# Conv-attention hybrid with a recurrence: the last half image in written order, and the recurrence on the attention loop's PSUM banks

## The chip, the cores and the metric

The kernel runs on one core of a Trainium2 chip. The metric is device time in microseconds (us) of one execution. A core has five engines with a queue each: TensorE (matmuls and transposes, PE in the profile; its weight loads are PEld), VectorE (DVE), ScalarE (ACT), GpSimd (POOL) and SyncE (SP), whose queue issues the transfers here. Matmuls write to PSUM[...]; all else lies in SBUF or in device memory.

## The reference, cut to what matters

The input x is four images of 128 channels by 64 x 64 pixels. There are two layers of attention and then a recurrence.

- Layer 0: group norm over x; queries, keys, values and a gate from 1x1 convolutions; softmax attention over the 4096 pixels; the result times the gate, projected, added to x.
- Layer 1: the pixels as 4096 tokens of 128 values. `q = LN(t) @ W`, scores `q @ q.T` (symmetric), softmax, product with LN(t), added to t.
- Recurrence: `Wx = LN(t) @ W.T`, batch norm over all tokens of all images, then `y = sigmoid(wx + y @ V.T)` over the tokens in order; y is added to t, and t goes out as an image.

The batch norm needs the mean and variance over all tokens. So the recurrence can't start before the last tokens of the last image have their Wx.

## The kernel before, in words

Everything is fp32. `fast` does the work; `general` is a slower path taken only when a check at the end fails, and it doesn't run in these measurements. An image is cut into `NB = 8` blocks of 512 tokens.

**Layer 1** (`layer1`) goes through the blocks in the order 6, 7, 5, 4, 3, 2, 1, 0. For block n it computes scores against the blocks a = n, n-1, ..., 0 only, in two steps i of 256 tokens each: scores (L685), exponential on ScalarE (L689), products with LN(t) (`direct`, L564), two steps behind. In the step with a = n and i = 1 half of the scores are had by transposing earlier ones (`quarter`, L537, L543, L547, L551). Since the scores are symmetric, the exponentials for a < n are also transposed (L692 on VectorE, then 16 transfers, L719) and used for block a (`reversed_products`, L577). Each partial sum is added into `oacc` on VectorE (`part`, L586). When block n has all its parts, `finish(n)` requests the old tokens (L614) and puts closures into a queue `pending`:

- `tokens`: four transposes on TensorE (L619), row sums and reciprocal (L622 to L624), the addition to the old tokens (L626), and a layer norm (`layernorm`: L294 and L295 for each quarter, `inv_sqrt` on GpSimd with L140 and L141, then L298);
- `turn`: four transposes (L639), a copy on ScalarE (L640), and `result` (transposition L270 and four transfers, L274) for the new tokens;
- `inputs`: a matmul (L648), its statistics for the batch norm (L649) and a copy into `wxs` (L652).

One closure is taken from the queue per step of the loop. For the last image, block 0 takes block 1's part directly (`order`, `turns`), so its two a are 0 and 1, and no transposed scores are needed there. At the end `flush()` runs what is left.

**PSUM.** In the loop three pools share the eight banks: `ps_s` (2 tiles of 2 banks, scores), `ps_o` (3 banks, products) and `ps_m` (1 bank, the closures). One closure with a tile in `ps_m` must have been read out before the next can write there. Block 0 of the last image takes banks of `ps_s` instead. Then the pools close, and `ps_r` with six banks opens for the recurrence.

**The recurrence** starts from 128 places at once, 32 tokens apart, each with W = 12 tokens of run-in, for the two halves of the images in turn: 44 steps. At each step VectorE writes `gain * wx` into a bank two steps ahead (`preload`, L838; three banks per half in turn), TensorE adds `V y` to it (L851), and ScalarE takes the sigmoid with the bias (L855). Step 0 needs no matmul (L848). [...]each bank is first marked with a matmul (L815) whose value doesn't matter. Ahead of it stand the batch norm's sums (L819, `inv_sqrt`, L821 to L824). From step 15 on VectorE also adds y to the tokens (L865, one per step), and after the last step the four images go out (L870). The checks follow: sums in range (`ok`, L794 to L796, placed before the recurrence) and the run-in long enough (`gap`, L874 to L877).

**Order.** The kernel is written in a layer that places the waits itself and plans the order of the instructions on each engine from estimated times. What is written earlier tends to go first, but an instruction that isn't ready in the plan is passed by later ones.[...] `tc.keep_in_program_order` pins single instructions. `tc.manual_schedule()` keeps everything inside it in written order on each engine; work written ahead of it can still be mixed in by the planner.

Of the kernel before, what the change touches and what calls it, by code (L numbers as in the profile page):

```python
# [23 lines left out]
NT = N // P  # L24
EPS_GN, EPS_LN, EPS_BN = 1e-5, 1e-5, 1e-5
# [4 lines left out]
QB = 512  # L30
NB = N // QB
# [5 lines left out]
G = N // L  # L37
GB = QB // L


DEN_LO, DEN_HI = 2.0**-60, 2.0**100
# [4 lines left out]
SQ, BQ, SK, BK, SG, BG, GAMMA, BETA = range(8)  # L46
# [121 lines left out]
def fast(  # L168
# [13 lines left out]
    with ExitStack() as st:  # L182
# [2 lines left out]
        accp = st.enter_context(tc.tile_pool(name="accp", bufs=1))  # L185
        work = st.enter_context(tc.tile_pool(name="work", bufs=1))
        stat = st.enter_context(tc.tile_pool(name="stat", bufs=4))
        ps_s = st.enter_context(tc.tile_pool(name="ps_s", bufs=2, space=PSUM))
        ps_o = st.enter_context(tc.tile_pool(name="ps_o", bufs=3, space=PSUM))
        ps_m = st.enter_context(tc.tile_pool(name="ps_m", bufs=1, space=PSUM))  # L190

# [13 lines left out]
        def flush(until=None):  # L205

            while pending and until not in done:
                pending.popleft()()
# [75 lines left out]
            nc.sync.dma_start(dst, via)  # L284

        n_moves = 0

        def layernorm(src, dst):
# [21 lines left out]
        def quarters(t):  # L310
            return [t[:, j, :].rearrange("q (p i) -> q p i", p=4) for j in range(NQ)]
# [198 lines left out]
        def layer1(b, h, qt):  # L510

            oacc = big.tile([P, NB, QB], F32, tag="oacc", name="oacc")
# [80 lines left out]
            def finish(n):  # L595
                cs = bass.ts(n, QB)
                rinv = stat.tile([P, NQ], F32, tag="rinv", name="rinv")
                t = work.tile([P, 4, NQ, 32], F32, tag="t", name="t1", bufs=2)
                if b == B - 1 and n == 0:

                    one, two = (ep.tile([P, 2, QB], F32, tag="e", name="last") for _ in range(2))
                    h2, t1 = (one[:, r, :].rearrange("q (j c) -> q j c", j=NQ) for r in range(2))
                    th = two[:, 0, :]

                    def bank():
                        return ps_s.tile([P, 2, QB], F32, tag="s", name="ml")[:, 0, :]
                else:
                    h2 = work.tile([P, NQ, C], F32, tag="h2", name="h2")
                    th = work.tile([P, QB], F32, tag="th", name="th")
                    t1 = work.tile([P, NQ, C], F32, tag="og", name="t1b")  # L610

                    def bank():
                        return ps_m.tile([P, QB], F32, tag="m", name="m1")
                nc.sync.dma_start(t, t_d[b, n])  # L614

                def tokens():
                    m = bank().rearrange("q (j c) -> q j c", j=NQ)
                    for j in range(NQ):
                        nc.tensor.transpose(m[:, j, :], oacc[:, n, bass.ts(j, P)], ident)  # L619
                    at = (B + b) * NT + n * NQ  # L620
                    den = den_all[:, at : at + NQ]
                    nc.vector.tensor_reduce(den, m, AX.X, ALU.add)  # L622
                    nc.vector.tensor_scalar(den, den, 1.0 / C, None, ALU.mult)
                    nc.vector.reciprocal(rinv, den)  # L624
                    for j in range(NQ):
                        nc.vector.scalar_tensor_tensor(  # L626
                            t1[:, j, :].rearrange("q (p i) -> q p i", p=4),
                            m[:, j, :].rearrange("q (p i) -> q p i", p=4), rinv[:, j : j + 1],
                            t[:, :, j, :], ALU.mult, ALU.add,
                        )  # L630
                    layernorm(quarters(t1), quarters(h2))

                def result():
                    turn_out(t1.rearrange("q j (p i) -> q j p i", p=4), t2_d[b, :, cs])

                def turn():
                    m = bank()
                    for j in range(NQ):
                        nc.tensor.transpose(m[:, bass.ts(j, P)], h2[:, j, :], ident)  # L639
                    nc.scalar.copy(  # L640
                        th.rearrange("c (p j k) -> c j p k", j=NQ, p=4),
                        m.rearrange("c (j p k) -> c j p k", j=NQ, p=4),
                    )
                    result()

                def inputs():
                    m = bank()
                    nc.tensor.matmul(m, lhsT=wt["f"], rhs=th, start=True, stop=True)  # L648
                    nc.vector.bn_stats(bn_st[:, b * NB + n, :], m)  # L649
                    m = m.rearrange("p (g i s) -> p i g s", i=L // 2, s=2)  # L650
                    if b == B - 1:
                        nc.vector.tensor_copy(wxs[:, :, b, bass.ts(n, GB), :], m)  # L652
                    else:
                        wx = work.tile([P, L // 2, GB, 2], F32, tag="wx", name="wx")
                        nc.vector.tensor_copy(wx, m)
                        nc.sync.dma_start(wxs_d[b, :, :, bass.ts(n, GB), :], wx)

                if b == B - 1 and n == 0:
                    pending.appendleft(tokens)
                    pending.extend([turn, inputs])  # L660
                elif b == B - 1 and n < 4:
                    pending.extend([tokens, turn, inputs])
                else:
                    pending.extend([tokens, nothing, nothing, nothing, turn, inputs])


            for n in [NB - 2, NB - 1] + list(range(NB - 3, -1, -1)):
                o = None
                flush((b, n))
                if n == NB - 2:  # L670
                    queries(n)
# [51 lines left out]
            while fifo:  # L723
                direct()
            pending.extend([reversed_products] * len(turned))

        def own_bank(_):
            return ps_m.tile([P, 512], F32, tag="m", name="mp")
# [44 lines left out]
        for b in range(B):  # L773
# [13 lines left out]
            while ahead:  # L787
                ahead.popleft()()
        flush()


        tc.keep_in_program_order(nc.scalar.activation(first_y, shift, AF.Sigmoid))
        ok = big.tile([P, 2, 2 * B * NT], F32, tag="oacc", name="ok")
        nc.vector.tensor_scalar(ok[:, 0, :], den_all, DEN_LO, None, ALU.is_ge)  # L794
        nc.vector.tensor_scalar(ok[:, 1, :], den_all, DEN_HI, None, ALU.is_le)
        nc.vector.tensor_reduce(par_ok[:, 1:2], ok.rearrange("p a b -> p (a b)"), AX.X, ALU.min)  # L796


    with ExitStack() as st:
        scan = st.enter_context(tc.tile_pool(name="scan", bufs=1))  # L800
        ps_r = st.enter_context(tc.tile_pool(name="ps_r", bufs=1, space=PSUM))
# [9 lines left out]
        HB = B // 2  # L811
        banks = [[ps_r.tile([P, 512], F32, tag=f"r{s}{i}", name="ps_r") for i in range(3)] for s in range(2)]
        for s in range(2):
            for i in range(3):
                nc.tensor.matmul(  # L815
                    banks[s][i][:, : HB * G], lhsT=ident, rhs=wxs[:, 0, :HB, :, 0],
                    start=True, stop=True, skip_group_check=True,
                )
        nc.vector.bn_aggr(mv, bn_st.rearrange("p a b -> p (a b)"))  # L819
        inv_sqrt(gain, mv[:, 1:2], EPS_BN)  # L820
        nc.vector.tensor_mul(gain, gain, col(GAMMA))  # L821

        nc.vector.tensor_mul(bias, mv[:, 0:1], gain)
        nc.vector.tensor_sub(bias, col(BETA), bias)  # L824
# [18 lines left out]
        for k, i in enumerate(steps):  # L843
# [15 lines left out]
            if k >= W:  # L859
                todo.extend((i - 3, b) for b in range(B) if i % 4 == 3)  # L860
                for j in range(len(todo) if i == L - 1 else min(1, len(todo))):
# [7 lines left out]
                    if i0 == L - 4:  # L869
                        nc.sync.dma_start(out[b], t2[:, b, :])  # L870


        gap = scan.tile([P, B, G - 1], F32, name="gap")
        nc.vector.tensor_sub(gap, state[:, :, 1:G], at(y, L - 1, slice(0, B))[:, :, : G - 1])  # L874
# [406 lines left out]
```

## Time and profile before

| | us |
|---|---|
| median of 3 runs | 3050.52 (3049.5 to 3051.89) |
| span of the profiled run | 3049.4 |
| TensorE busy | 2991.0 (98%) |
| VectorE busy | 1676.6 (55%) |
| last attention product ends (L564) | 2945.1 |
| last inputs matmul (L648) | 2957.4 to 2959.5 |
| marks of the six banks (L815) | 2960.9 to 2966.1 |
| recurrence's matmuls (L851) | 2966.0 to 3022 |
| output transfers issued (L870) | from 3023.2 |
| end | 3049.4 |

Times in the lower half are positions in the span. The profile lists busy time per engine, the granted TensorE clock and the share of the transfer engines by stretch of the span, and a timeline of instructions with the idle time of the engine before each and what ended it.

### The profile page before, as it was taken

How to read it: one execution, taken by the hardware profiler on the slowest of the kernel's cores; microseconds unless marked ns; L12 is line 12 of the kernel's file. 1: busy time of each engine (PE TensorE's matmuls, PEld its weight loads, DVE VectorE, ACT ScalarE, POOL GpSimd, SP SyncE). 2: the span in 40 equal slices, each digit the busy share in tenths (PEclk: the TensorE clock that was granted, in tenths of full speed). 3: DMA queues.
4: the chain of work that ended last, by engine and by line, in shares of the span. 5: the costliest groups of instructions: out<-in, count | busy, mean ns of one | idle time of the engine just before them, and what ended most of it. 6: DMA issues, size and time to landing. Idle time of an engine off the chain costs nothing.

```text
span 3049.4 us, 31514 instructions
## 1 busy us (share of the span) xinstructions
PE 2991.0 (98%) x10716; PEld 1370.4 (45%) x10716; DVE 1676.6 (55%) x3114; ACT 1032.5 (34%) x1149; POOL 218.4 (7%) x215
## 2 busy tenths in 40 slices
PE   8999999999999999999999999999999999999985
PEld 4444444444444444444444444444444444444442
DVE  6666654434666664443466665443456666333356
ACT  3444432222344433222244443222234443222224
POOL 0011100000011100000011011000001111000000
PEclk9999999999999999999999999999999999999988
DMA  1112143434111123343311114343422112544333
GB/s 42 38 56 56 48 116 88 96 88 101 45 56 56 44 87 97 91 101 84 89 45 56 39 49 117 85 98 89 99 59 56 42 49 88 144 99 103 96 115 155
DMA packets 247562, 241.09 MB, mean 79 GB/s; under 512 B 90080, under 2 KB 162272, under 8 KB 246368
## 3 DMA queue, kind: packets, MB, share of 16 engines
q1 hardware_dynamic: 247392, 238.98, 29.4%
q8 instruction: 88, 1.44, 0.2%
q14 instruction: 82, 0.67, 0.1%
HBM read 65.80 MB, written 56.62 MB: 40 GB/s over the span
## 4 chain that ended last, share of the span: by engine, by line
PE 93%; DVE 3%; SPq 2%; ACT 1%; DMA 1%; issue 0%; POOL 0%; DVEq 0%; ACTq 0%
PE o L437 28%; PE o L564 15%; PE ps L233 14%; PE ps L685 14%; PE ot L577 12%; SPq L719 2%; PE m L262 1%; PE m L648 1%; PE mp L400 1%; PE ps L537 1%; PE mp L365 1%; PE mq L529 1%; PE mp L385 1%; DVE t2s L865 1%; DVE ps_r L838 1%; PE m L639 1%
## 5 line engine op out<-in xcount | busy, mean ns | idle before, releaser
L437 PE MATMUL o<-e,nxt 64*128 64x512 f32 x4096 | 972.9, 589 | 0.0
L235 ACT ACTIVATE e<-ps 128x1024 f32<-128x1024 f32 x512 | 521.6, 1025 | 688.7 <-PE ps L233 646.7
L242 DVE TENSOR_TENSOR acc<-acc,e 128x1024 f32<-128x1024 f32 x448 | 547.0, 1221 | 231.3 <-ACT e L235 215.0
L437 PEld LDWEIGHTS o<-e,nxt 64*128 64x128 f32 x4096 | 403.3, 187 | 483.0 <-issue 474.2
L233 PE MATMUL ps<-nxt 64*128 64x512 f32 x2048 | 542.4, 595 | 2.0 <-DVE nxt L377 0.9
L564 PE MATMUL o<-e,h 128*128 128x512 f32 x1160 | 537.0, 592 | 0.0
L689 ACT ACTIVATE e<-ps,shift 128x1024 f32<-128x1024 f32 x258 | 287.4, 1114 | 646.6 <-PE ps L685 357.1
L685 PE MATMUL ps<-qt 128*128 128x512 f32 x1032 | 482.9, 594 | 2.7 <-ACT qt L530 2.7
L577 PE MATMUL ot<-tt,h 128*128 128x512 f32 x888 | 400.9, 593 | 0.0
L692 DVE STREAM_TRANSPOSE dd<-e 128x512 f32<-128x512 f32 x444 | 281.7, 682 | 138.0 <-ACT e L689 103.0
L564 PEld LDWEIGHTS o<-e,h 128*128 128x128 f32 x1160 | 218.8, 190 | 268.3 <-issue 268.0
L233 PEld LDWEIGHTS ps<-nxt 64*128 64x128 f32 x2048 | 198.2, 187 | 232.0 <-issue 148.5
L685 PEld LDWEIGHTS ps<-qt 128*128 128x128 f32 x1032 | 189.9, 190 | 219.3 <-issue 190.3
L577 PEld LDWEIGHTS ot<-tt,h 128*128 128x128 f32 x888 | 167.8, 190 | 210.2 <-issue 205.1
L586 DVE TENSOR_TENSOR oacc<-oacc,ot 128x512 f32<-128x512 f32 x87 | 59.7, 686 | 288.2 <-PE ot L577 288.2
L140 POOL TENSOR_SCALAR rstd<-mv 128x4 f32<-128x4 f32 x64 | 14.6, 228 | 2380.0 <-DVE mv L295 2380.0
L491 DVE SCALAR_TENSOR_TENSOR t<-yt,rinv,t 128x128 f32<-128x128 f32 x128 | 36.4, 346 | 77.4 <-DMA yt<-turn_d 77.4
L502 POOL TENSOR_SCALAR h<-h 128x512 f32<-128x512 f32 x32 | 72.4, 2261 | 63.8 <-DVE d L270 61.7
L454 POOL TENSOR_SCALAR xb<-xb,bpc 128x512 f32<-128x512 f32 x32 | 59.1, 1846 | 245.0 <-DMA xb<-in_x_dram 211.5
L547 ACT ACTIVATE e<-ps,shift 128x512 f32<-128x512 f32 x32 | 22.0, 687 | 143.8 <-PE ps L543 126.3
L141 POOL TENSOR_TENSOR rstd<-rstd,mhalf 128x4 f32<-128x4 f32 x64 | 66.4, 1037 | 5.3
L588 DVE COPY oacc<-ot 128x512 f32<-128x512 f32 x24 | 16.6, 692 | 85.1 <-PE ot L577 85.0
(156 smaller groups left out, 1609.1 us busy)
## 6 DMA issues: line engine op xcount, KB each, us to landing
tt<-dd SPq DMA_DIRECT2D x1776, 64.0 KB, 2.0
turn_d<-d SPq DMA_DIRECT2D x384, 64.0 KB, 1.8
xb<-in_x_dram SPq DMA_DIRECT2D x32, 256.0 KB, 3.2
t<-turn_d SPq DMA_DIRECT2D x32, 256.0 KB, 2.7
yt<-turn_d SPq DMA_DIRECT2D x32, 256.0 KB, 2.6
t_d<-t SPq DMA_DIRECT2D x32, 256.0 KB, 2.0
qt<-turn_d SPq DMA_DIRECT2D x32, 256.0 KB, 2.9
t<-t_d SPq DMA_DIRECT2D x32, 256.0 KB, 3.0
```

Of the source, the lines that this page charges most:

```text
L141: nc.gpsimd.tensor_tensor(dst, dst, mhalf[:, :n], ALU.pow)
L233: nc.tensor.matmul(ps[:, h, :], lhsT=lhsT, rhs=rhs, start=True, stop=True)
L235: nc.scalar.activation(e, ps, AF.Exp, scale=scale)
L242: nc.vector.tensor_tensor(acc, acc, e, ALU.add)
L437: nc.tensor.matmul(o[r], lhsT=v[rs, p + h * PAIRS, :], rhs=e[rs, h, :], start=(p == 0 and h == 0), stop=(p == PAIRS - 1 and h == 1),)
L502: nc.gpsimd.tensor_scalar(hn, hn, 1.0, None, ALU.add)
L564: nc.tensor.matmul(o, lhsT=h[:, NQ * a + 2 * i + half, :], rhs=e[:, half, :], start=(a == order(n)[0] and i == 0 and half == 0), stop=(a = ...
L577: nc.tensor.matmul(ot, lhsT=h[:, NQ * n + j, :], rhs=t[:, :, j, :, :].rearrange("q p k j -> q k p j"), start=(j == 0), stop=(j == NQ - 1),)
L685: nc.tensor.matmul(ps[:, half, :], lhsT=qt[:, bass.ts(at, P)], rhs=qt[:, bass.ts(n, QB)], start=True, stop=True,)
L689: nc.scalar.activation(e, ps, AF.Exp, bias=shift)
L692: nc.vector.transpose(d.rearrange("q f b k j -> q k b f j")[:, 2 * i + half], e[:, half, :].rearrange("q (b f j) -> q b f j", b=NQ, f=NQ),)
L719: nc.sync.dma_start(t[bass.ts(f, 32), p], d[bass.ts(p, 32), f])
```

## The change

It has four parts.

1. From block 0 of the last image on, and through the recurrence, everything is put in written order (`tc.manual_schedule`). For block 1 an empty closure is put between `tokens` and `turn`.
2. The three PSUM pools live until the end, and the recurrence takes its six banks from them. Four are marked in block 0's `tokens`, while VectorE and GpSimd work on the layer norm; two after the last `inputs`, followed by three wider matmuls of the same kind, which keep TensorE busy. Block 0's closures take banks of `ps_o`.
3. The batch norm's sums come directly after the last statistics. The last copy into `wxs` is put behind the start of `inv_sqrt` on GpSimd.
4. The check of the sums (`ok`) moves from before the recurrence to the very end.

It is for the stretch between the last attention product and the recurrence, where the engines wait for each other.

```diff
-        ps_s = st.enter_context(tc.tile_pool(name="ps_s", bufs=2, space=PSUM))
+        ps_s = keep_ctx.enter_context(tc.tile_pool(name="ps_s", bufs=2, space=PSUM))
...
                     def bank():
-                        return ps_s.tile([P, 2, QB], F32, tag="s", name="ml")[:, 0, :]
+                        return ps_o.tile([P, QB], F32, tag="o", name="ml")
...
+                    if b == B - 1 and n == 0:
+                        for i in (1, 2):
+                            tile_ = ps_s.tile([P, 2, QB], F32, tag="s", name="ps_r")
+                            for r in range(2):
+                                banks[r][i] = tile_[:, r, :]
+                                mark(banks[r][i])
                     layernorm(quarters(t1), quarters(h2))
...
-                    if b == B - 1:
+                    if b == B - 1 and n == 0:
+                        last_inputs.append(m)
+                    elif b == B - 1:
                         nc.vector.tensor_copy(wxs[:, :, b, bass.ts(n, GB), :], m)
...
+                elif b == B - 1 and n == 1:
+                    pending.extend([tokens, nothing, turn, inputs])
...
+                if b == B - 1 and n == 0:
+                    keep_ctx.enter_context(tc.manual_schedule())
                 flush((b, n))
...
+        def mark(m, cols=HB * G):
+            nc.tensor.matmul(
+                m[:, :cols], lhsT=ident, rhs=oacc_all[:, 1, :cols], start=True, stop=True,
+                skip_group_check=True,
+            )
...
         flush()
-        tc.keep_in_program_order(nc.scalar.activation(first_y, shift, AF.Sigmoid))
-        ok = big.tile([P, 2, 2 * B * NT], F32, tag="oacc", name="ok")
-        nc.vector.tensor_scalar(ok[:, 0, :], den_all, DEN_LO, None, ALU.is_ge)
...
+        banks[0][0] = ps_o.tile([P, QB], F32, tag="o", name="ps_r")
+        banks[1][0] = ps_m.tile([P, QB], F32, tag="m", name="ps_r")
+        for r in range(2):
+            mark(banks[r][0])
+        for _ in range(3):
+            mark(banks[0][0], QB)
+        nc.scalar.activation(first_y, shift, AF.Sigmoid)
+        nc.vector.bn_aggr(mv, bn_st.rearrange("p a b -> p (a b)"))
+        inv_sqrt(gain, mv[:, 1:2], EPS_BN)
+        nc.vector.tensor_copy(wxs[:, :, B - 1, :GB, :], last_inputs[0])
+        nc.vector.tensor_mul(gain, gain, col(GAMMA))
...
-        for s in range(2):
-            for i in range(3):
-                nc.tensor.matmul(
-                    banks[s][i][:, : HB * G], lhsT=ident, rhs=wxs[:, 0, :HB, :, 0],
...
-        nc.vector.bn_aggr(mv, bn_st.rearrange("p a b -> p (a b)"))
...
+        ok = scan.tile([P, 2, 2 * B * NT], F32, name="ok")
+        nc.vector.tensor_scalar(ok[:, 0, :], den_all, DEN_LO, None, ALU.is_ge)
```

More of the change, by code (lines that the diff above doesn't have):

```diff
@@ L187, in fast @@
         stat = st.enter_context(tc.tile_pool(name="stat", bufs=4))
-        ps_s = st.enter_context(tc.tile_pool(name="ps_s", bufs=2, space=PSUM))
-        ps_o = st.enter_context(tc.tile_pool(name="ps_o", bufs=3, space=PSUM))
-        ps_m = st.enter_context(tc.tile_pool(name="ps_m", bufs=1, space=PSUM))
+        ps_s = keep_ctx.enter_context(tc.tile_pool(name="ps_s", bufs=2, space=PSUM))
+        ps_o = keep_ctx.enter_context(tc.tile_pool(name="ps_o", bufs=3, space=PSUM))
+        ps_m = keep_ctx.enter_context(tc.tile_pool(name="ps_m", bufs=1, space=PSUM))
         ahead: deque = deque()
@@ L286, in fast @@
         n_moves = 0
+        oacc_all = None
         def layernorm(src, dst):
@@ L510, in layer1 @@
         def layer1(b, h, qt):
-            oacc = big.tile([P, NB, QB], F32, tag="oacc", name="oacc")
+            nonlocal oacc_all
+            oacc = oacc_all = big.tile([P, NB, QB], F32, tag="oacc", name="oacc")
             dd = big.tile([P, 2, NQ, NQ, NQ, 32], F32, tag="dd", name="dd")
@@ L725, in layer1 @@
             pending.extend([reversed_products] * len(turned))
+        HB = B // 2
+        banks = [[None] * 3 for _ in range(2)]
+        last_inputs = []
+        def mark(m, cols=HB * G):
[3 more added lines that the diff above has]
+            )
         def own_bank(_):
@@ L789, in fast @@
         flush()
-        tc.keep_in_program_order(nc.scalar.activation(first_y, shift, AF.Sigmoid))
-        ok = big.tile([P, 2, 2 * B * NT], F32, tag="oacc", name="ok")
-        nc.vector.tensor_scalar(ok[:, 0, :], den_all, DEN_LO, None, ALU.is_ge)
-        nc.vector.tensor_scalar(ok[:, 1, :], den_all, DEN_HI, None, ALU.is_le)
-        nc.vector.tensor_reduce(par_ok[:, 1:2], ok.rearrange("p a b -> p (a b)"), AX.X, ALU.min)
+        banks[0][0] = ps_o.tile([P, QB], F32, tag="o", name="ps_r")
[9 more added lines that the diff above has]
+        nc.vector.tensor_mul(gain, gain, col(GAMMA))
+        nc.vector.tensor_mul(bias, mv[:, 0:1], gain)
+        nc.vector.tensor_sub(bias, col(BETA), bias)
     with ExitStack() as st:
         scan = st.enter_context(tc.tile_pool(name="scan", bufs=1))
-        ps_r = st.enter_context(tc.tile_pool(name="ps_r", bufs=1, space=PSUM))
         t2 = scan.tile([P, B, N], F32, name="t2s")
@@ L807, in fast @@
         nc.gpsimd.memset(state[:, :, 0:1], 0.0)
-        HB = B // 2
-        banks = [[ps_r.tile([P, 512], F32, tag=f"r{s}{i}", name="ps_r") for i in range(3)] for s in range(2)]
-        for s in range(2):
-            for i in range(3):
-                nc.tensor.matmul(
-                    banks[s][i][:, : HB * G], lhsT=ident, rhs=wxs[:, 0, :HB, :, 0],
-                    start=True, stop=True, skip_group_check=True,
-                )
-        nc.vector.bn_aggr(mv, bn_st.rearrange("p a b -> p (a b)"))
[L820 to L824, printed above, removed]
         halves = [slice(s * HB, (s + 1) * HB) for s in range(2)]
@@ L870, in fast @@
                         nc.sync.dma_start(out[b], t2[:, b, :])
+        ok = scan.tile([P, 2, 2 * B * NT], F32, name="ok")
+        nc.vector.tensor_scalar(ok[:, 0, :], den_all, DEN_LO, None, ALU.is_ge)
+        nc.vector.tensor_scalar(ok[:, 1, :], den_all, DEN_HI, None, ALU.is_le)
+        nc.vector.tensor_reduce(par_ok[:, 1:2], ok.rearrange("p a b -> p (a b)"), AX.X, ALU.min)
         gap = scan.tile([P, B, G - 1], F32, name="gap")
```

## The prediction

> **What bounds the kernel now.** I read the page first, then the busy time of each engine by stretch at the end of the run, then the timeline of those stretches, and the chain of waits last, to see which waits carry the end.
>
> ```profile
> PE 2991.0 (98%) x10716; PEld 1370.4 (45%) x10716; DVE 1676.6 (55%) x3114; ACT 1032.5 (34%) x1149; POOL 218.4 (7%) x215
> ```
>
> TensorE is busy nearly all the time, and none of its matmuls goes away. So the change can only pay where TensorE is not the bound: after the last attention product. Each row below is a stretch, its length, the busy time of PE, PEld, DVE, ACT and POOL, the granted clock, the DMA share and GB/s.
>
> ```profile
> 2928.90:2945.10 16.20, 16.18 (x47) 7.40 (x45) 10.28 (x37) 3.98 (x5) 1.50 (x3) 1.00 0.12 32
> 2945.10:2959.50 14.40, 6.77 (x16) 2.48 (x16) 8.89 (x31) 2.66 (x4) 2.31 (x3) 0.62 0.15 36
> 2959.50:2966.00 6.50, 5.08 (x13) 4.02 (x14) 4.77 (x11) 1.13 (x2) 0.92 (x3) 0.52 0.86 325
> 2985.30:3025.00 39.70, 33.79 (x112) 17.23 (x112) 39.51 (x85) 27.56 (x57) 0.00 (x0) 1.00 0.03 14
> 3025.00:3049.40 24.40, 0.19 (x2) 0.12 (x2) 2.70 (x7) 0.00 (x0) 0.00 (x0) 0.54 0.81 326
> ```
>
> The reader is to see five regimes. TensorE is full until 2945.1. From there to 2966.0 (20.9 us) no engine is full and the clock falls to about half: a serial chain. The recurrence follows; from 2985.3 VectorE is full (39.51 of 39.70). In the last 24.4 us only the output moves. The timeline has the serial chain and what precedes it (start, duration, engine, line; in brackets the idle time before).
>
> ```profile
> 2922.26 0.69 DVE L586 TENSOR_TENSOR oacc<-oacc,ot 128x512 f32<-128x512 f32 x1 [7.48 <-PE ot L577]
> 2929.13 0.69 DVE L586 TENSOR_TENSOR oacc<-oacc,o 128x512 f32<-128x512 f32 x1 [6.18 <-PE o L564]
> 2929.73 1.12 DVE L626 SCALAR_TENSOR_TENSOR t1b<-m,rinv,t 128x128 f32<-128x128 f32 x4
> ...
> 2945.12 0.69 DVE L586 TENSOR_TENSOR oacc<-oacc,o 128x512 f32<-128x512 f32 x1 [0.37 <-PE o L564]
> ...
> 2948.45 1.90 PE L648 MATMUL m<-th,w 128*128 128x512 f32 x2 [0.73 <-ACT th L640]
> 2950.39 0.70 DVE L649 BATCH_NORM_STATS2 bn_st<-m 128x6 f32<-128x512 f32 x1 [1.08 <-PE m L648]
> 2951.01 0.67 DVE L652 COPY wxs<-m 128x512 f32<-128x512 f32 x1
> 2951.60 0.34 DVE L626 SCALAR_TENSOR_TENSOR last<-ml,rinv,t 128x128 f32<-128x128 f32 x1
> ...
> 2957.38 2.07 PE L648 MATMUL ml<-last,w 128*128 128x512 f32 x2 [0.67 <-ACT last L640]
> 2960.92 5.21 PE L815 MATMUL ps_r<-wxs,ident 128*128 128x256 f32 x12 [1.47 <-DVE wxs L652]
> ```
>
> Two losses show. The fourth L626 of block 0 stands in VectorE's queue behind L649 and L652 of block 1, so it starts at 2951.60 instead of about 2949.3. And the six bank marks (L815, two passes each) run at half clock directly ahead of the recurrence. Of the 20.9 us, the chain of waits gives 5.2 to L815.
>
> [...]L648 takes 1.10 us at 2937.53 but 2.07 at 2957.38, and the marks take 5.21/12 = 0.43 us a pass, all at half.[...]
>
> **The change part by part.** Call E the end of the last L564 (2945.1 now) and S the first recurrence matmul L851 (2966.0). I price E to S, then E itself.
>
> *E to S.* In written order nothing of block 1 is left after E. Block 0's chain: L586 0.7 and four transposes 0.7 = 1.4; L622, L623, L624 and four L626 are 0.7 + 0.2 + 0.2 + 1.2 = 2.3; four pairs of L294 and L295, now alternating so that each L295 waits for its L294, about 4 x 0.37 = 1.5 (now 1.66 with L270 in front of the last L295; L270 goes behind the copy); POOL's L140 and L141 with hand-overs 1.45 (from 2944.76 to 2946.20 in the chain); L298 and the transposes behind it 1.5; L640 0.65. Sum 8.8. L648 is 1.1 at full or 2.1 at half clock. Four marks now lie behind the tokens' transposes, while VectorE works; at full clock 4 x 2 x 0.22 = 1.8 us. They keep TensorE busy until about E + 3.2, and then it idles to E + 7:[...] I take half clock, 2.1. L648 ends at E + 10.9 (full clock: 9.9).
>
> Then L649 0.7, L819 1.0, POOL's pair 1.0 (it hides the copy L652, 0.67, which stood on the path), three small operations with hand-overs 0.6: 3.3; half a step of L848 0.6: 3.9. Beside it TensorE runs 2 marks of 256 columns and 3 of 512, 2048 columns. From L815 (1536 columns in 5.21 at half clock) that is 6.9 at half and 3.5 at full clock;[...] I take 4.3, and that, not 3.9, sets S. E to S = 10.9 + 4.3 = 15.2, against 20.9: 5.7 less. At full clock all through 9.9 + 3.9 = 13.8 (7.1 less); all at half 10.9 + 6.9 = 17.8 (3.1 less).
>
> *E.* Block 1's turn (0.44) and inputs (0.9), which ran after E, now precede the last two products: +1.35.[...] Block 1's transposes wait for L586: 0.7, with all of block 0's scores behind them. Then tokens to turn is 0.64 + 2.3 + 1.5 + 1.45 + 0.4 = 6.3, and TensorE has 0.44 + 1.3 (quarter) + 1.72 (scores) + 1.72 (two products) = 5.2 to fill it: 1.1. Together +3.15, if block 2 is out of the way in time.
>
> *After S.* From 2985.3 VectorE is the bound, with 32 x 0.6 (L865) and 27 x 0.79 (pairs of L838) whatever the order; written order may save the 0.2 of idleness at 2990. Take -0.2. A shift of S reaches the end one for one. The check of sums (0.26 + 0.25 + 0.69) moves behind the last L865; the output transfers, which run some 20 us longer, hide it. The t2 loads (last landing 22.4 us after issue) now wait for the marks, because these read oacc, whose memory is reused. The first L865 comes 19.3 us after S and the fourth 23.4: just enough, 0 to 0.5 us. The sigmoid table (1.28) stays hidden behind L648.
>
> Sum: -5.7 + 3.15 - 0.2 + 0.2 = -2.6: **3050.5 - 2.6 = about 3048**.
>
> **Rivals.**
> *A late block 2.* Block 1's transposes need the single ps_m bank, which block 2 holds from its tokens to its inputs. Now VectorE's order puts block 2's L626 behind block 1's L586 (2929.13), though its operand was requested at 2921.1 and such loads land in 2.9 us. Today TensorE fills the 11.1 us from there to block 1's transposes (2940.19) with block 0's scores and products. In written order those stand behind these transposes, so only a reversed product (3.4), block 2's turn and inputs (1.4) are left. The chain from L586 at about 2928.3 takes 0.7 + 1.1 + 1.6 + 1.5 + 0.4 + 1.0 + 0.6 + 1.1 + 1.3 = 9.3. Hole 4.5, and E slips by 3.15 + 4.5 = 7.6: -5.7 + 7.6 = +1.9, and a clock that falls in the hole adds about 1: 3053. For it: the order in the trace. Against it: block 2's L626 could go ahead once block 0 no longer competes; the planner decides that.
> *No holes and a warm clock.* +1.35 - 7.1 - 0.2 = -6.0: 3044.5. Against it: 1.1 and 0.7 us of waits are in the written order itself[...].
> *Slower by much.* The hole of the late block 2, with TensorE at half clock for the 14 us of work after it (up to +5), or t2 loads that hold up VectorE (+1): 3050.5 + 1.9 + 5 + 1 = about 3058. For it: the clock falls now in the 2945 to 2959 stretch with 6.77 us of 14.40 busy.
>
> **How the numbers follow.** Forecast (a few us faster, 3045 to 3050) 0.44; late block 2 (3050 to 3056) 0.25; no holes 0.17, put below 3044.4 for its chance although its worked-out time is at that edge; much slower 0.14. 0.2% is 6.1 us. So faster 0.17, same 0.69, slower 0.14. The predicted time is the forecast's, 3048. The range 3043 to 3056 takes in the first two cases and most of the third and leaves out the last.
>
> **What would show it.** E to S of 14 to 16 us; no matmul mark between L648 and the recurrence but the five; L626 of block 0 unbroken; L652 of block 0 after L819, under POOL. TensorE's idle time between 2925 and E tells the forecast (about 2) from the late block 2 (over 5). I'm wrong if the work before 2900 is planned otherwise too, if the copy or the marks hold up L848, or if the first L865 waits for its load.

## The result and the profile after

The changed kernel takes 3070.22 us (median of 4 runs, 3069.79 to 3070.63) against 3050.84 for the kernel before (4 runs): a ratio of 1.0064, 95% interval 1.0046 to 1.0081. It is 19.4 us slower; the forecast was 2.5 us faster, and the time lies above its range of 3043 to 3056.

The page of the kernel after, busy time of each engine:

```profile
PE 2994.7 (98%) x10722; PEld 1373.8 (45%) x10722; DVE 1681.5 (55%) x3114; ACT 1030.6 (34%) x1149; POOL 218.2 (7%) x215
```

TensorE does 3.7 us more, with six passes more. Work didn't grow by 19 us; waiting did. The busy time by stretch of the kernel after (stretch, length, busy PE, PEld, DVE, ACT, POOL, granted clock, DMA share, GB/s):

```profile
2928.30:2940.00 11.70, 7.74 (x20) 3.36 (x19) 6.46 (x21) 0.58 (x1) 1.26 (x2) 0.79 0.09 22
...
2954.70:2971.90 17.20, 10.79 (x28) 5.91 (x28) 11.28 (x33) 2.73 (x5) 2.18 (x5) 0.80 0.06 16
...
2996.00:3043.00 47.00, 33.16 (x113) 17.93 (x112) 42.50 (x85) 27.24 (x57) 0.00 (x0) 1.00 0.02 6
3043.00:3068.50 25.50, 0.19 (x2) 0.11 (x2) 4.45 (x11) 0.00 (x0) 0.00 (x0) 0.53 0.79 323
```

Before, TensorE had 0.02 us idle in the 16 us ahead of E; now it is idle for 3.96 of 11.70 us. The stretch from E to S has become shorter. In the recurrence VectorE did fill 39.51 of 39.70 us; now it has 85 instructions again, spread over 47 us, and is idle for 4.5 us. The last stretch is the output, as before. The timeline of the kernel after, in the same three places:

```profile
2928.41 0.69 DVE L588 TENSOR_TENSOR oacc<-oacc,o 128x512 f32<-128x512 f32 x1 [6.18 <-PE o L566]
2929.01 1.12 DVE L628 SCALAR_TENSOR_TENSOR t1b<-m,rinv,t 128x128 f32<-128x128 f32 x4
...
2933.66 1.10 PE L648 MATMUL m<-ident,h 128*128 128x128 f32 x4 [1.85 <-DVE h L299]
...
2935.48 2.07 PE L657 MATMUL m<-th,w 128*128 128x512 f32 x2 [0.73 <-ACT th L649]
...
2938.94 1.12 PE L621 MATMUL m<-ident,oacc 128*128 128x128 f32 x4 [1.38 <-DVE wxs L663]
...
2957.34 1.13 DVE L628 SCALAR_TENSOR_TENSOR last<-ml,rinv,t 128x128 f32<-128x128 f32 x4
...
2963.91 2.08 PE L657 MATMUL ml<-last,w 128*128 128x512 f32 x2 [0.73 <-ACT last L649]
...
2965.78 5.30 PE L752 MATMUL ps_r<-oacc,ident 128*128 128x256 f32 x10
...
2969.18 0.16 DVE L834 TENSOR_TENSOR bias<-par,bias 128x1 f32<-128x1 f32 x1
...
2971.24 1.11 ACT L867 ACTIVATE y<-wxs,bias,gain 128x256 f32<-128x256 f32 x2 [5.87 <-DVE ps_r L857]
...
2972.67 0.49 ACT L874 ACTIVATE y<-ps_r,bias 128x256 f32<-128x256 f32 x1 [0.31 <-PE ps_r L870]
2973.20 1.17 PE L870 MATMUL ps_r<-y,w 128*128 128x256 f32 x4 [0.58 <-ACT y L874]
...
2977.99 1.17 PE L870 MATMUL ps_r<-y,w 128*128 128x256 f32 x4 [0.58 <-ACT y L874]
...
2979.27 1.01 DVE L857 TENSOR_SCALAR ps_r<-wxs,gain 128x256 f32<-128x256 f32 x2 [1.26 <-ACT y L874]
2979.74 2.47 PE L870 MATMUL ps_r<-y,w 128*128 128x256 f32 x8 [0.58 <-ACT y L874]
```

The reader is to see three things. First, blocks 2 and 1 follow one another with TensorE waiting at L648, L657 and L621, the last for the copy that frees the `ps_m` bank. Second, the bias is ready at 2969.34 (L834), yet step 0 (L867) starts at 2971.24, when the marks (L752) have ended. (The profile puts this wait down to the preload, L857; the two runs with the marks on `wxs` and on `oacc`, below, show that it is the marks.) Third, in step 1 the matmul of half 1 (L870 at 2973.20) needs `y` of step 0 only, which was ready at 2972.35, but it starts after half 0's sigmoid of the same step (2972.67 + 0.49 = 2973.16). From then on the pattern repeats every three steps in 4.80 us, from 2973.20 over 2977.99 to 2982.79: 1.60 a step.

For comparison, this is how the recurrence begins in the kernel before, with TensorE's thirteen matmuls unbroken:

```profile
2965.97 4.27 PE L851 MATMUL ps_r<-y,w 128*128 128x256 f32 x13
```

With E and S as in the prediction (last product's end, first recurrence matmul), the time splits as follows. The recorded spans don't all begin at the same point of the program (up to 4 us apart). So each E is shifted by as much as brings the first batch-norm statistics to 524.5, near where they stand in the kernel before (524.54); the two other columns don't depend on it.

| kernel | E | E to S | S to end | median |
|---|---|---|---|---|
| before | 2945.0 | 20.9 | 83.4 | 3050.84 |
| after | 2954.5 | 17.2 | 96.6 | 3070.22 |
| difference | +9.4 | -3.7 | +13.2 | +19.4 |

The differences add up to 18.9, near the 19.4 between the medians. The largest stands where the prediction had put nothing: after S.

### The profile page after: what moved, and what is told of

Same layout as the page of the kernel before. It is cut to its first block, busy times and chain, and to the rows that moved or that the text cites. A ratio compares the mean times of both kernels' runs of the same rounds, so it can differ in the third digit from the quotient of the medians.

```text
span 3068.5 us, 31479 instructions
## 1 busy us (share of the span) xinstructions
PE 2994.7 (98%) x10722; PEld 1373.8 (45%) x10722; DVE 1681.5 (55%) x3114; ACT 1030.6 (34%) x1149; POOL 218.2 (7%) x215
## 4 chain that ended last, share of the span: by engine, by line
PE 93%; DVE 2%; SPq 2%; ACT 1%; DMA 1%; issue 0%; POOL 0%; DVEq 0%; ACTq 0%
PE o L438 28%; PE o L566 15%; PE ps L233 14%; PE ps L701 14%; PE ot L579 12%; SPq L735 2%; ACT y L874 1%; PE m L262 1%; PE ps_r L870 1%; PE m L657 1%; PE mp L401 1%; PE mp L366 1%; PE mq L531 1%; PE ps L539 1%; PE mp L386 1%; PE m L648 1%
## 5 line engine op out<-in xcount | busy, mean ns | idle before, releaser
L701 PE MATMUL ps<-qt 128*128 128x512 f32 x1032 | 482.9, 594 | 2.7 <-ACT qt L532 2.7
L701 PEld LDWEIGHTS ps<-qt 128*128 128x128 f32 x1032 | 189.8, 190 | 218.8 <-issue 190.8
L870 PE MATMUL ps_r<-y,w 128*128 128x256 f32 x168 | 49.9, 416 | 19.7 <-ACT y L874 16.7
```

Source lines behind the costliest of these rows:

```text
L701: nc.tensor.matmul(ps[:, half, :], lhsT=qt[:, bass.ts(at, P)], rhs=qt[:, bass.ts(n, QB)], start=True, stop=True,)
L870: nc.tensor.matmul(bank(k, s), lhsT=wt["vt"], rhs=before, start=False, stop=True, skip_group_check=True,)
```

## The experiments

There were two questions: why a step of the recurrence takes longer, and why E comes late. My reading of the first was that the halves wait for each other through the shared tiles of `ps_s`; of the second, the late block 2. Where an expectation numbers its theories, the first is the reading held at that time and the others are rivals. The measured terms of all runs stand in a table at the end of this section. Line numbers of the edited kernels are shifted by a few.

### Which part of the change costs what

**Banks paired by half.** The two banks that share a tile of `ps_s` go to one half of the images, instead of one to each half. In the change, a tile held bank i of half 0 and of half 1.

```diff
-                        for i in (1, 2):
+                        for r in range(2):
                             tile_ = ps_s.tile([P, 2, QB], F32, tag="s", name="ps_r")
-                            for r in range(2):
-                                banks[r][i] = tile_[:, r, :]
+                            for i in (1, 2):
+                                banks[r][i] = tile_[:, i - 1, :]
                                 mark(banks[r][i])
```

> The changed kernel, with one edit: the two banks of a ps_s tile go to the same half (step residues 1 and 2) and no longer to the two halves. Theory 1 (a tile shared by the halves makes half 1's matmul and VectorE's preload wait for ScalarE's reading of half 0): steps of the recurrence fall from 1.60 to 1.30 us, the stretch from the first recurrence matmul to the end from 96.6 to about 83.5 us, and the time from 3070 to about 3057. Rival (written order on all engines is what paces the recurrence): steps stay at 1.60 and the time at 3070.

3062.86 us. E and E to S stay; S to end falls from 96.6 to 89.2, just over half of the loss. What is left shows on the timeline of this kernel:

```profile
2996.95 3.74 PE L870 MATMUL ps_r<-y,w 128*128 128x256 f32 x12 [0.88 <-DVE ps_r L857]
```

Now it is the preload, into the other bank of the tile, that meets the sigmoid of its own half, and every third step waits 0.88 us: 4.62 us for three steps (2996.95 to 3001.57).

**The same sharing alone, in the kernel before.** Three tiles of two banks take the place of six of one; the banks, the order and the marks stay.

```diff
-        banks = [[ps_r.tile([P, 512], F32, tag=f"r{s}{i}", name="ps_r") for i in range(3)] for s in range(2)]
+        shared = [ps_r.tile([P, 2, 512], F32, tag=f"r{i}", name="ps_r") for i in range(3)]
+        banks = [[shared[i][:, s, :] for i in range(3)] for s in range(2)]
```

> The kernel before, with one edit: the six recurrence banks are three tiles of two banks, one bank for each half, instead of six tiles. Theory 1: here all three residues are shared (in the changed kernel two of three are), so each step takes about 1.75 us instead of 1.30, 43 steps, less what VectorE's limit of 1.38 takes back in the later steps: +13 to +20 us, 3064 to 3071. Rival (written order or the pools' lives): no change, 3051.

3070.4 us: 19.3 us lost by this edit alone, all of it after S. Its timeline:

```profile
2970.24 1.17 PE L852 MATMUL ps_r<-y,w 128*128 128x256 f32 x4 [0.58 <-ACT y L856]
...
2971.51 1.01 DVE L839 TENSOR_SCALAR ps_r<-wxs,gain 128x256 f32<-128x256 f32 x2 [0.74 <-ACT y L856]
2971.99 1.17 PE L852 MATMUL ps_r<-y,w 128*128 128x256 f32 x4 [0.58 <-ACT y L856]
```

Every step now takes 1.75 us, with TensorE waiting 0.58 for ScalarE in each. The wait is thus one for the tile, not for the bank: the same six banks in six tiles had no such wait.

**The change without written order.**

```diff
-                if b == B - 1 and n == 0:
-                    keep_ctx.enter_context(tc.manual_schedule())
```

> The changed kernel without the written-order region; banks, marks and all else as changed, tiles shared by the halves. Theory 1: the recurrence keeps its 1.60 us steps, since the wait is one of data; only the hole of the late block 2 goes, so the last attention product ends near 2945 instead of 2954.7, and the time is about 3070 - 9 = 3061. Rival (written order paces the recurrence): steps of 1.30 us, and the time about 3070 - 9 - 13 = 3048.

E is back at 2945.1, which answers where the 9.4 us come from. The time isn't: 3079.19, in four runs 3081.97, 3078.79, 3079.59 and 3063.21. Only the last is near what theory 1 gives. The busy time by stretch of this kernel:

```profile
2980.00:3000.00 20.00, 17.13 (x36) 9.40 (x34) 7.78 (x17) 8.25 (x17) 0.00 (x0) 0.50 0.42 178
...
3020.00:3050.00 30.00, 21.72 (x74) 11.68 (x73) 26.23 (x55) 17.74 (x38) 0.00 (x0) 1.00 0.00 1
```

For some 48 us of the recurrence (2971.5 to 3019.3) the clock stays at 0.50, with TensorE recorded idle for 2.87 of 20.00 us. The mean clock of the whole execution was 0.985 or 0.986 in the three long runs and 0.994 in the fourth. Once the clock is back, three steps take 4.79 us (L867 at 3025.83 and again at 3030.62), as in the kernel after: the wait for the tile is there without written order too, as theory 1 says. The load of ScalarE's sigmoid table isn't pinned here, so it comes at the last moment (1.28 us, TensorE idle 2.31). The recurrence begins at 2969.15 with the clock still at 1.00, and 2.3 us later the clock falls. Why it falls there and stays down isn't shown by these runs.

**Paired by half, and written order only from the last `flush`.** The edit of the first experiment, and:

```diff
-                if b == B - 1 and n == 0:
-                    keep_ctx.enter_context(tc.manual_schedule())
...
+        keep_ctx.enter_context(tc.manual_schedule())
         flush()
```

> As pair_by_half, and the written-order region starts only behind block 0's last product, at the last flush. Theory 2 (the slip of the last product from 2945.1 to 2954.7 comes from written order inside block 0's loop: block 1's transposes stand ahead of block 0's scores and wait for block 2): the last product ends at 2945 to 2947, the time is about 3057 - 9 = 3048. Rival (the longer lives of the PSUM pools and the banks of ps_o for block 0 cause the slip): it stays near 2954 and the time near 3057.

3055.38: E is 2945.0 again, and 7.5 us come back against the paired kernel. So written order up to the last product cost more than it brought.

### Six tiles, and where written order may begin

**Six banks in six tiles.** One bank of each `ps_s` tile, three of `ps_o`, and `ps_m`; block 0's closures make do with a `ps_o` bank and `ps_m`. The mark of the `ps_m` bank therefore comes behind the last copy into `wxs` (not in the lines below).

```diff
-                        for i in (1, 2):
-                            tile_ = ps_s.tile([P, 2, QB], F32, tag="s", name="ps_r")
...
+                        for r in range(2):
+                            banks[r][1] = ps_s.tile([P, 2, QB], F32, tag="s", name="ps_r")[:, 0, :]
+                            mark(banks[r][1])
+                        for r in range(2):
+                            banks[r][2] = ps_o.tile([P, QB], F32, tag="o", name="ps_r")
+                            mark(banks[r][2])
```

> The changed kernel, with the recurrence's six banks in six tiles (one bank of each ps_s tile, three of ps_o, ps_m); block 0's closures use the third ps_o bank and ps_m. Theory 1 (a shared tile is the only thing that slows the steps): steps of 1.30 us and 83.5 us from the first recurrence matmul to the end; time 3070 - 13 = 3057, about 6 below pair_by_half, where half of the waits stayed. Rival (part of the slow steps in pair_by_half comes from written order on VectorE, preload ahead of the addition): steps stay near 1.5 us and the time near 3062.

3056.56. S to end is 82.4, less than before the change, and the timeline has the matmuls unbroken:

```profile
2972.50 9.78 PE L875 MATMUL ps_r<-y,w 128*128 128x256 f32 x30 [0.83 <-ACT y L872]
```

The whole loss after S was the tiles. What is left, +6.1 us in the median, is for the most part E's 9.4 less the 3.5 gained in E to S and 1.0 after S.

**Written order already from block 1.** Six tiles, and `n == 1` in place of `n == 0` for the beginning.

> As six_tiles, and the written-order region starts one block earlier, at block 1. Theory 2 (the hole ahead of block 1's transposes comes from block 2's closures, which the planner puts behind block 1's sum on VectorE): in written order block 2's tokens go ahead of that sum, the hole shrinks from some 6 us to 1 or 2, and the last product ends near 2948 instead of 2954.7; time about 3057 - 6 = 3051. Rival (written order itself makes TensorE stand, whoever holds the bank): the end of the last product stays at 2954 or comes later, and the time is 3057 or more.

3065.35, worse: E comes 8.8 us later still. The timeline:

```profile
2924.52 1.12 DVE L632 SCALAR_TENSOR_TENSOR t1b<-m,rinv,t 128x128 f32<-128x128 f32 x4 [8.97 <-DMA t<-t_d]
...
2929.21 1.15 PE L653 MATMUL m<-ident,h 128*128 128x128 f32 x4 [10.07 <-DVE h L299]
```

In written order block 2's tokens are waited for by its turn (L653), with block 1's scores behind that; and the tokens' load was issued late, at 2921.49, behind transfers of transposed exponentials in SyncE's queue. So what was to make room for block 2 made TensorE wait 10 us for it.

**A bank of its own for block 1.** Six tiles, and block 1's closures take `ps_o` banks, so they needn't wait for block 2 to leave `ps_m`.

```diff
+                        if b == B - 1 and n == 1:
+                            return ps_o.tile([P, QB], F32, tag="o", name="m1")
```

> As six_tiles, and block 1's closures of the last image take banks of ps_o instead of the single ps_m. Theory 2 (block 1's transposes wait for ps_m, which block 2 holds until its inputs are read out): the wait ahead of block 1's transposes falls to the 0.7 us of its own sum, and the last product ends 4 to 6 us earlier than 2954.7; time 3051 to 3053. Rival (they wait for VectorE, which is in block 2's layer norm): no change, 3057.

3054.11: E improves by 3.0 of the 9.4 us only. The timeline shows what follows:

```profile
2941.78 1.24 PE L655 MATMUL m<-ident,h 128*128 128x128 f32 x4 [2.23 <-DVE h L299]
...
2942.81 3.21 PE L708 MATMUL ps<-qt 128*128 128x512 f32 x4
```

Block 1's transposes go early, but VectorE does the two layer norms in turn. So block 1's turn waits 2.23 us, and the scores behind it take 3.21 us for four (1.88 for four in the kernel after, L701 at 2942.16, where the clock was 1.00). The single bank is a third of the cause; in written order the next wait takes its place.

**Six tiles, late order, marks that read `wxs`.** Written order from the last `flush`, as above, and:

```diff
-                m[:, :cols], lhsT=ident, rhs=oacc_all[:, 1, :cols], start=True, stop=True,
+                m[:, :cols], lhsT=ident, rhs=wxs[:, 0, :HB].rearrange("p b g s -> p (b g s)")[:, :cols], start=True, stop=True,
```

> As six_tiles, the written-order region only from the last flush, and the marks read wxs instead of oacc, whose memory the recurrence's tiles reuse. Expected from the earlier runs: last product near 2945 as before, 1.30 us steps, and the recurrence's first sigmoid no longer held until the marks end (it started 2.3 us after its bias was ready in pairs_late_order). pairs_late_order's 3055.4, less 5 for the steps, less 0.2 to 1 for the marks (TensorE itself still has to finish them): about 3050, level with the kernel before. If it is under 3047, the marks held up more than their own TensorE time.

3048.26. E is back at 2945.0, E to S stays at 17.6 and S to end at 82.9: the loss ahead of E is gone, and what was gained behind it is kept.

### The rest, each part alone

**Marks back on `oacc`.** As the last one, with `oacc` read as in the change.

> As six_tiles_late_marks_wxs, but the marks read oacc again, as in the change. Theory 3 (the tiles of the recurrence reuse oacc's memory, so its first sigmoid and the loads of the tokens wait until the last mark has read it): the first sigmoid starts with the end of the marks, and the recurrence 0.7 to 2.2 us later; time 3049 to 3050.5. Rival (the marks' source is indifferent): 3048.3.

3049.27. In E to S it is 1.85 us slower (19.48 for 17.63). The medians say less: they differ by 1.0, and as distances from the kernel before on each run's own chip (1.9 and 2.2 us) by 0.3. The timeline of the kernel with marks on `wxs`:

```profile
2959.34 4.51 PE L754 MATMUL ps_r<-wxs,ident 128*128 128x256 f32 x10
...
2963.06 1.13 ACT L870 ACTIVATE y<-wxs,bias,gain 128x256 f32<-128x256 f32 x2 [4.13 <-DVE bias L837]
```

The timeline of the one with marks on `oacc`:

```profile
2958.94 5.41 PE L754 MATMUL ps_r<-oacc,ident 128*128 128x256 f32 x10
...
2964.51 1.12 ACT L870 ACTIVATE y<-wxs,bias,gain 128x256 f32<-128x256 f32 x2 [5.97 <-DVE ps_r L860]
```

With `wxs` step 0 starts when the bias is ready, beside the marks. With `oacc` it starts after them, since `y` lies in memory that `oacc` had. The bias itself is ready 16.8 us after E in both.

**Without the three wide marks.** The first late kernel (marks on `wxs`), less these lines:

```diff
-        for _ in range(3):
-            mark(banks[0][0], QB)
```

> As six_tiles_late_marks_wxs, without the three wide marks. If they only delay: the recurrence starts at the same time or 0.5 us earlier, time 3048. If they bring the clock back (theory 4): TensorE is at half clock in the first steps, which then take about 1.7 us (0.87 us for a half's two passes at half clock instead of 0.45) until the clock returns; some 3 to 10 steps of it, +1 to +5 us, 3049 to 3053; more if the clock doesn't return, as in planner_order.

3050.15, 1.9 us slower in the median (1.2 as distances from the kernel before on each chip). The busy time by stretch of this kernel, without them:

```profile
2962.70:2968.00 5.30, 4.21 (x11) 2.38 (x12) 4.17 (x12) 2.76 (x6) 0.36 (x2) 0.74 0.94 396
```

The same stretch of the kernel with them:

```profile
2962.70:2968.00 5.30, 5.09 (x18) 2.46 (x16) 4.64 (x13) 3.97 (x8) 0.00 (x0) 1.00 0.98 417
```

E to S is the same 17.63 in both, but the stretch with the first steps has a mean clock of 0.74: without the wide marks the clock is back at 2961.7, falls again at 2965.2, 0.8 us after S, and returns at 2968.6. So it comes back without the wide marks too, against theory 4; with them it is 1.00 all through this stretch. S to end is 84.58 against 82.86: the three matmuls, whose values nobody reads, pay for themselves by 1.7 us in the traces. In the times this isn't settled: the intervals of the two ratios overlap.

**Written order alone, in the kernel before.** The two lines of `manual_schedule`, and nothing else of the change; the single pin of the sigmoid's table load is left out, since the region keeps it in order.

> The kernel before, with one edit: the written-order region from block 0 of the last image to the end (banks, marks, copies and checks as before, no empty closure for block 1). If written order inside block 0's loop is what makes the last product late: it ends 9 us later as in the changed kernel, and some 3 more because block 1's turn stands one step nearer to its tokens, so near 2958; from there to the recurrence 17 to 19 us instead of 20.9; the recurrence keeps 1.30 us steps; time 3058 to 3062. If the slip comes from the changed banks: no change of the last product, and about 3048.

3062.89. E comes 14.1 us later, more than in the change, which has the empty closure between block 1's tokens and turn (block 0's banks differ too; the two weren't tried apart). Its timeline:

```profile
2939.22 1.12 PE L619 MATMUL m<-ident,oacc 128*128 128x128 f32 x4 [1.38 <-DVE wxs L652]
...
2946.21 1.16 PE L639 MATMUL m<-ident,h 128*128 128x128 f32 x4 [3.31 <-DVE h L298]
2947.15 3.62 PE L687 MATMUL ps<-qt 128*128 128x512 f32 x4
```

The late block 2 is there as in the change (1.38 at L619), and block 1's turn waits 3.31 us where the change had 0.17. Behind E, written order alone shortens the way to the recurrence from 20.9 to 18.1 us: that is 2.8 of the 3.7 us that the whole change gains there.

**Block 1's inputs behind block 0's layer norm.** The late kernel with marks on `wxs`, with block 1's `inputs` two places later, and in block 0's layer norm all statistics ahead of the aggregates. Block 0's `turn` takes a `ps_o` bank instead of `ps_m`, which block 1's `inputs` now hold longer (not in the lines below).

```diff
-                    pending.extend([tokens, nothing, turn, inputs])
+                    pending.extend([tokens, nothing, turn, nothing, nothing, inputs])
...
-                nc.vector.bn_aggr(mv[:, j, :], s6)
+                sums.append(s6)
+                if not first:
+                    nc.vector.bn_aggr(mv[:, j, :], s6)
+            for j in range(NQ if first else 0):
+                nc.vector.bn_aggr(mv[:, j, :], sums[j])
```

> As six_tiles_late_marks_wxs, and block 1's inputs run behind block 0's layer norm (its statistics and copy took 1.3 us of VectorE ahead of that layer norm), and in that layer norm the four statistics go ahead of the four aggregates (they alternate now, 1.55 us; back to back some 1.15). Expected: the last product unchanged, from it to the recurrence 17.6 - 1.3 - 0.4 = 15.9 us, time 3046.5.

3047.0 (20 runs), ratio 0.9988, 95% interval 0.9981 to 0.9995: the fastest, some 4 us below the kernel before, and the only one whose interval lies clear of 1 on the fast side. The timeline:

```profile
2950.94 0.86 DVE L296 BATCH_NORM_STATS2 s<-last 128x6 f32<-128x128 f32 x4
2951.72 0.36 DVE L301 BATCH_NORM_AGGREGATE mv<-s 128x2 f32<-128x6 f32 x4
```

Statistics and aggregates take 1.14 us from first to last, where in turn they take 1.68 (2958.38 to 2960.06 in the kernel after, 2952.00 to 2953.68 in the kernel that this one edits). Block 1's statistics and copy, which stood in VectorE's queue between block 0's addition to the old tokens and this layer norm, now come after it. E to S is 16.1. The two edits weren't tried apart.

All runs (E, E to S, S to end from the profiled execution; the ratio is to the kernel before on the same chip):

| kernel | E | E to S | S to end | median | ratio, 95% interval |
|---|---|---|---|---|---|
| pair_by_half | 2954.5 | 17.3 | 89.2 | 3062.86 | 1.0037 (1.0023 to 1.0051) |
| before_shared_tiles | 2945.0 | 20.3 | 102.8 | 3070.4 | 1.006 (1.0043 to 1.0077) |
| planner_order | 2945.1 | 19.9 | 111.1 | 3079.19 | 1.0072 (1.0045 to 1.01) |
| pairs_late_order | 2945.0 | 19.8 | 88.4 | 3055.38 | 1.0014 (1.0005 to 1.0022) |
| six_tiles | 2954.5 | 17.4 | 82.4 | 3056.56 | 1.002 (1.0013 to 1.0027) |
| six_tiles_order_from_1 | 2963.2 | 16.9 | 82.8 | 3065.35 | 1.0046 (1.0029 to 1.0063) |
| six_tiles_bank_for_1 | 2951.5 | 17.0 | 82.8 | 3054.11 | 1.0011 (1.0003 to 1.002) |
| six_tiles_late_marks_wxs | 2945.0 | 17.6 | 82.9 | 3048.26 | 0.9993 (0.9987 to 1.0) |
| six_tiles_late_marks_oacc | 2945.0 | 19.5 | 82.8 | 3049.27 | 0.9994 (0.9985 to 1.0003) |
| late_no_wide_marks | 2945.1 | 17.6 | 84.6 | 3050.15 | 0.9996 (0.9988 to 1.0005) |
| before_written_order | 2959.2 | 18.1 | 83.2 | 3062.89 | 1.0038 (1.0024 to 1.0052) |
| late_deferred_inputs | 2945.0 | 16.1 | 82.7 | 3047.0 | 0.9988 (0.9981 to 0.9995) |

## Why the prediction was wrong, step by step

***After S*: "A shift of S reaches the end one for one."** This step failed, and it is the one that made the prediction wrong: -0.2 was priced, +13.2 measured. The prediction counted VectorE's instructions in the recurrence "whatever the order" and took the banks to be the same six. It read part 2 of the diff as a matter of when the banks are marked, and didn't ask which waits the new tiles bring: `banks[r][i] = tile_[:, r, :]` puts the halves, which run against each other, into one tile. Then matmul, sigmoid and preload of one half wait for those of the other. A step costs 1.60 us instead of 1.30 (56 us of L851 by 43 steps); 43 x 0.30 = 13, the measured loss. Shown both ways: sharing alone brings it into the kernel before, six tiles take it out of the change. None of the rivals had it; "slower by much" was built on the clock and the `t2` loads.

**E: +3.15 "if block 2 is out of the way in time".** It wasn't: the rival of a late block 2 is what happened, by the chain that the prediction gave, L586 to block 1's transposes, with 10.5 us (2928.41 to 2938.94) for the 9.3 worked out. The term was mis-sized: E slipped by 9.4, not 7.6. TensorE idles for 3.96 us in the hole (4.5 predicted) and 0.17 ahead of block 1's turn (1.1 predicted). But the clock, priced at 1 us, costs about 2.4. It falls from 1.00 to 0.50 at 2935.1, behind block 2's turn, and is back at 2941.9; against the kernel before the inputs take 2.07 us and not 1.10, block 1's transposes 1.12 and not 0.60, and the quarter's scores behind them (L539) 1.92 and not 1.03. Block 2's turn takes 1.10 and not 0.60 at full clock still, because its four transposes follow the four quarters of the layer norm (L299, 1.11 us from 2933.25) as VectorE finishes them: 0.5 more. Block 1's turn and inputs add about 1.7 (1.35 predicted). That is 8.7 of the 9.4. So the chance was too low rather than the picture wrong. The profile of before showed what it hung on (block 2's L626 behind L586, and what TensorE did meanwhile), and the prediction leaned on a planner that might decide otherwise; the order came out unchanged. The kernels without written order ahead of E have it back at 2945, and written order alone moves it in the kernel before: the cause is written order. The runs with the bank and with block 1 show that no single wait explains the whole slip.

**E to S: 15.2 predicted, 17.2 measured.** Up to the end of the last inputs (L657) it is right: E + 11.3 for E + 10.9, at a clock of 0.50 (2.08 us), which the prediction had taken as an estimate, with the fourth L626 unbroken and the copy under GpSimd. Then 5.9 instead of 4.3. The marks took 5.3 us and not the 4.3 taken, about midway between the 3.5 and 6.9 estimated from L815 for full and half clock: the clock came back at 2969.2, with the marks running from 2965.78 to 2971.08. And S came 0.8 after their end, because step 0 had to wait for them. The prediction saw that reuse of `oacc`'s memory for the `t2` loads, and missed it for `y`. With marks that read `wxs`, step 0 no longer waits. That the clock would fall while TensorE idles, and how soon it would be back, was the author's estimate: the lines that the prediction gives show the two speeds (L648 in 1.10 and in 2.07 us), and not when they change. The last section has what the traces show.

**Parts that held.** The check of sums at the end is hidden by the output. L626 doesn't wait for block 1's statistics any more. The early marks and the written order behind E do shorten E to S, by 3.7 us in the change, of which written order alone gives 2.8. (What a bank without its mark would do isn't shown: every kernel here marks all six.) With the order from the last `flush` only, block 1's inputs stand behind E again, and it is 3.3 with marks on `wxs` and 1.4 with marks on `oacc`. With the tiles mended but the late block 2 left, the change would have ended at 3056.56, just outside the range.

What stays open: the interval of the kernel with late order and marks on `wxs` touches 1.0, so its gain of some 2 us is likely and not certain. How much the source of the marks is worth in the median isn't settled either: 1.85 us in the traces, 0.3 to 1.0 in the medians. The same holds for the three wide marks: 1.7 us in the traces, 1.2 in the medians as distances.

## What to carry to other kernels

When a change gives a buffer's job to another pool, look at which accesses then share one tile, and not only at when the buffer comes free: where the waits are placed by tile, two independent chains in one tile run in turn, which cost more here (13.2 us) than the late last product (9.4 us). Begin a stretch of written order behind the last place where the planner fills a hole, since there a wait held up what was queued behind it (10.07 us of TensorE at L653, with the order begun at block 1). And work through the rival that your own profile lines speak for before you set the chance on a planner's goodwill.

## What the runs showed that was not expected

- TensorE's busy share didn't tell by itself which clock was granted. (The times at which the clock changes between 1.00 and 0.50 are worked out from its means over stretches.) In the kernel before it fell at 2948.7, when TensorE hadn't been idle for more than 0.78 us at a time since E and had been busy for 1.89 of the 3.70 us from 2945.0; it returned at 2965.7, 4.8 us after the marks began. In the kernel in the planner's order TensorE was recorded busy for 17.13 of 20.00 us at a clock of 0.50, and it stayed so for some 48 us; in the kernel after, with 33.16 busy of 47.00 us, it was 1.00. (The first stretch has 36 passes and the second 113; two passes of 128x512, L648 of the kernel before, took 1.10 us at 1.00 and 2.07 at 0.50.) A clock that fell in the first steps of the recurrence was back at 2968.6 after 2965.2 in the kernel without the wide marks, and at 3019.3 after 2971.5 in the one in the planner's order.
- Three matmuls without use, beside the batch norm's sums, go with 1.7 us less after S in the traces (82.86 for 84.58) and with a higher clock in the first steps (1.00 for 0.74 over 5.30 us).
- VectorE's four pairs of statistics and aggregates (128x128 each) take 1.68 us when each aggregate follows its statistics, and 1.14 when all statistics go first.
